# Eight one-group loads of x that leave out DMA engine 4, in place of four two-group loads

## The chip, the cores and the metric

The kernel runs on one core of a Trainium2 chip. The metric is the device time of one execution in microseconds, taken as the median of several runs. The profile is of one further execution, with its own time.

## What is computed

The input `r_inputs` has 4096 rows of 32 fields with 64 numbers each, the weights `W` one 64 x 64 matrix for each of the 496 pairs of fields i < j. All is float32. Cut to what matters, the reference is:

```python
i_idx, j_idx = np.triu_indices(32, k=1)
vi = inputs[:, i_idx, :]
vj = inputs[:, j_idx, :]
vdotw = jnp.einsum('bpd,pde->bpe', vi, W)
inter = vdotw * vj
return inter.reshape(4096, -1)
```

So each pair (i, j) yields `(x_i @ W_ij) * x_j`, 64 numbers for each row, and the output, 4096 x 31744 floats or 520 MB, is far larger than the inputs.

## The kernel before

**Tiling.** The 4096 rows are cut into 8 chunks of 512 (`BANK`). The host lays x out transposed: two fields times 64 numbers make 128 partitions, and 16 such field pairs (`NPR`) of a chunk stand side by side in `xbuf`, 512 columns each. There is one `xbuf`, used again by every chunk. It is thought of as 4 groups of 4 field pairs (`GROUP`); a group takes 8,192 bytes in each partition, 1 MB in all.

**Steps.** `steps_of` lists 124 steps a chunk. The outer order is by the group of `p`, the field pair that is multiplied by weights: group 0 has 55 steps, group 1 has 39, group 2 has 23 and group 3 has 7. Within these, the field pair `q`, which is the other factor, runs over the same and the later groups. In one step, TensorE makes two PSUM banks of 128 x 512 (L218, or L208 for the pairs inside a field pair), and VectorE multiplies them by x into an output slot in SBUF (L236, or L228). Two neighbouring steps with the same `p` are made together where PSUM and the slot have room.

**Stores.** The output goes through three slots of 20, 18 and 18 banks (`SLOTS`). A full slot is stored with one DMA from ScalarE's queue (L180), 36,864 or 40,960 bytes a partition; a slot is written again only when its store has landed on all 16 DMA engines. The weights, 8.1 MB, are loaded once at the start from the same queue.

**Loads of x.** `x_loads` lists the loads: chunk 0 comes in three (groups 0; 1; 2 and 3), every later chunk in two (groups 0 and 1; 2 and 3). The load of the next chunk into a group is issued as soon as the last step with a `p` in that group is out, since no later step of the chunk reads it: for groups 0 and 1 together after 94 steps, for 2 and 3 at the chunk's end. Most loads go out from SP (L140): one DMA of 128 partitions, 8 for each of the 16 DMA engines.

**The light loads.** `is_light` picks some loads that go out from GpSimd instead and that put no data on DMA engine 4 (`LIGHT`). `load_beside` cuts such a load in two DMAs: partitions 0 to 119 as 15 lines of 8 on the 15 engines from 5 around to 3, and partitions 120 to 127 as 2 lines of 4 on the two engines from `PAIRS_FROM[lap]` on. On the host, every line is followed by 16 floats (`PAD`). [...]`from_engine` first issues a small DMA into `nudge`:

```python
k = (e - cursor) % DMA_ENGINES
if k:
    nudge = nudges[e == LIGHT + 1]
    from_pool(nudge[:k]..., x[: k * 8]...)
cursor = e
```

So one light load is four DMAs on GpSimd's queue: nudge, 2 lines, nudge, 15 lines. All four have line L99 in the profile. `keep_in_program_order` holds them in the order in which they are written. Before, the light loads are those of groups 0 and 1 of chunks 1, 3, 5 and 7.

**What sets the order.** [...] Every DMA engine carries stores, SP's loads and GpSimd's loads.

Of the kernel before, what the change touches and what calls it, by code (L numbers as in the profile page):

```python
# [18 lines left out]

DMA_ENGINES = 16  # L20
LIGHT = 4
LIGHT_CHUNKS = [1, 3, 5, 7]
PAIRS_FROM = [7, 15, 1, 7]
HEAD = P // DMA_ENGINES
REST = HEAD // 2
PAD = 16
# [27 lines left out]
def x_loads(B, NPR):  # L54

    loads = [(0, 0, 1), (0, 1, 2), (0, 2, 4)]
    for c in range(1, B // BANK):
        loads += [(c, 0, 2), (c, 2, 4)]
    return loads


def is_light(load):

    return load[1] == 0 and load[0] in LIGHT_CHUNKS


def load_size(load):

    pads = (DMA_ENGINES + 1) * PAD if is_light(load) else 0
    return P * (load[2] - load[1]) * GROUP * BANK + pads  # L70
# [3 lines left out]
def pair_bilinear_kernel(  # L74
# [22 lines left out]
    def from_pool(out, in_):  # L97

        tc.keep_in_program_order(nc.gpsimd.dma_start(out=out, in_=in_))  # L99

    def from_engine(e):

        nonlocal cursor
# [3 lines that stand above are left out]
            from_pool(  # L107
                nudge[:k].rearrange("p (h c) -> p h c", h=2)[:, :, :4],
                x[: k * 8].rearrange("(p h c) -> p h c", p=k, h=2),
            )  # L110
        cursor = e

    def load_beside(at, xt, n_row, lap):

        nonlocal cursor
        most = DMA_ENGINES - 1
        for e, k, rows, p in (
            (PAIRS_FROM[lap], 2, REST, most * HEAD),
            (LIGHT + 1, most, HEAD, 0),
        ):  # L120
            from_engine(e)
            n = rows * n_row
            lines = x[at : at + k * (n + PAD)].rearrange("(k c) -> k c", k=k)
            from_pool(xt[p : p + k * rows], lines[:, :n])
            at += k * (n + PAD)
            cursor = (e + k) % DMA_ENGINES

    xbuf = const.tile([P, NPR * BANK], F32, tag="x", name="x")
    loads = x_loads(B, NPR)

    def load_x(load):

        at = sum(load_size(before) for before in loads[: loads.index(load)])
        c, g0, g1 = load
        n = (g1 - g0) * GROUP * BANK
        xt = xbuf[:, g0 * GROUP * BANK : g0 * GROUP * BANK + n]
        if is_light(load):
            load_beside(at, xt, n, LIGHT_CHUNKS.index(c))
        else:
            nc.sync.dma_start(out=xt, in_=x[at : at + P * n].rearrange("(p c) -> p c", p=P))  # L140

    for load in loads:
        if load[0] == 0:
            load_x(load)
# [42 lines left out]
    for c in range(NC):  # L187
        todo = list(enumerate(steps))
        while todo:
# [6 lines left out]
            n = 1  # L196
# [52 lines left out]
            for load in loads:  # L249
                if last and load[0] == c + 1 and load[2] == p // GROUP + 1:  # L250
                    load_x(load)
# [58 lines left out]
```

## Time and profile before

| | |
|---|---|
| time, median of 3 runs | 1314.06 us (1312.31 to 1315.08) |
| profiled execution: its own time | 1312.53 us |
| profiled execution: span, first to last instruction | 1310.8 us |
| busy: TensorE matmuls / weight loads | 1055.3 us (81%) / 401.3 us (31%) |
| busy: VectorE | 1152.6 us (88%) |
| busy: GpSimd | 9.4 us (1%) |
| moved by DMA | 562.39 MB, mean 429 GB/s |
| read from HBM / written to HBM | 41.68 MB / 520.09 MB |
| DMAs of x from SP / from GpSimd, nudges with them | 13 / 16 |

Shares are of the span. "DMA" in the profile is the mean busy share of the 16 DMA engines, and a DMA queue's packets are what an engine moves in one piece; here, one partition's row of a transfer. In the table of waits, a line reads: engine and instruction that waited, what ended the wait, then the total in us, the number of waits, and the longest. In the list of DMA issues, a line has what is loaded or stored, the issuing queue, the number of DMAs, the size of each in KB and the median time from issue to landing in us.

### The profile page before, as it was taken

How to read it: one execution, taken by the hardware profiler on the slowest of the kernel's cores; microseconds unless marked ns; L12 is line 12 of the kernel's file. 1: busy time of each engine (PE TensorE's matmuls, PEld its weight loads, DVE VectorE, ACT ScalarE, POOL GpSimd, SP SyncE). 2: the span in 40 equal slices, each digit the busy share in tenths (PEclk: the TensorE clock that was granted, in tenths of full speed). 3: DMA queues.
4: the chain of work that ended last, by engine and by line, in shares of the span. 5: the costliest groups of instructions: out<-in, count | busy, mean ns of one | idle time of the engine just before them, and what ended most of it. 6: DMA issues, size and time to landing. Idle time of an engine off the chain costs nothing.

```text
span 1310.8 us, 9392 instructions
## 1 busy us (share of the span) xinstructions
PE 1055.3 (81%) x4096; PEld 401.3 (31%) x4096; DVE 1152.6 (88%) x725; POOL 9.4 (1%) x20
## 2 busy tenths in 40 slices
PE   6888787988778878888778887788788788878882
PEld 2333233323323323333233332333233333323330
DVE  6999799998899879998889998899889998799993
POOL 0000000000000000000000000000000000000000
PEclk9999899998999989999999999899989999999996
DMA  9999999999999999999999999999999999999998
GB/s 390 430 432 434 422 433 430 433 431 433 432 433 433 431 432 429 433 436 429 433 434 433 433 428 424 435 434 432 432 433 434 427 427 420 430 431 437 432 433 382
DMA packets 19625, 562.39 MB, mean 429 GB/s; under 512 B 2688, under 2 KB 2688, under 8 KB 2816
## 3 DMA queue, kind: packets, MB, share of 16 engines
q10 hardware_dynamic: 16560, 528.23, 93.6%
q1 hardware_dynamic: 1872, 25.17, 4.5%
q0 software_dynamic: 1152, 8.39, 1.6%
q8 instruction: 32, 0.52, 0.1%
q14 instruction: 9, 0.07, 0.0%
HBM read 41.68 MB, written 520.09 MB: 429 GB/s over the span
## 4 chain that ended last, share of the span: by engine, by line
DMA 55%; DVE 36%; PE 5%; issue 2%; DVEq 0%
DMA out_dram<-slot 54%; DVE slot L236 32%; PE pring L218 5%; DVE slot L228 3%; PE pring L208 1%; DMA w<-in_w_dram 1%; DVEq L236 0%; DVEq L298 0%; DVEq L228 0%
## 5 line engine op out<-in xcount | busy, mean ns | idle before, releaser
L236 DVE TENSOR_TENSOR slot<-pring,x 128x1024 f32<-128x1024 f32 (+1 forms) x661 | 1077.2, 1697 | 122.8 <-DMA out_dram<-slot 81.6
L218 PE MATMUL pring<-x,w 64*128 64x512 f32 x3840 | 993.2, 626 | 216.7 <-DVE slot L236 206.6
L218 PEld LDWEIGHTS pring<-x,w 64*128 64x128 f32 x3840 | 385.5, 191 | 824.6 <-DVE slot L236 508.5
L228 DVE TENSOR_TENSOR slot<-pring,x 64x1024 f32<-64x1024 f32 x64 | 77.9, 1217 | 13.2 <-PE pring L208 12.7
L208 PE MATMUL pring<-x,w 64*64 64x512 f32 x256 | 65.4, 631 | 14.0 <-DMA w<-in_w_dram 7.4
L208 PEld LDWEIGHTS pring<-x,w 64*64 64x64 f32 x256 | 15.7, 137 | 59.4 <-DVE slot L236 26.6
L99 POOL DMA_DIRECT2D x<-in_x_dram x8 | 4.7, 586 | 1078.3 <-DVE slot L236 1078.3
L99 POOL DMA_DIRECT2D nudge<-in_x_dram x8 | 4.6, 569 | 0.9 <-POOLq L294 0.9
L294 POOL MEMSET const-bfloat16-1.0<- 128x1 bf16 x1 | 0.1, 101 | 0.0
L294 POOL MEMSET const-float32-0.0<- 128x1 f32 x1 | 0.1, 98 | 0.2 <-issue 0.2
L294 POOL MEMSET const-float32-1.0<- 128x1 f32 x1 | 0.1, 98 | 0.0
L294 POOL MEMSET const-uint8-127<- 128x1 uint8 x1 | 0.1, 98 | 0.0
## 6 DMA issues: line engine op xcount, KB each, us to landing
out_dram<-slot ACTq DMA_DIRECT2D x68, 4608.0 KB, 23.6
out_dram<-slot ACTq DMA_DIRECT2D x35, 5120.0 KB, 22.6
x<-in_x_dram SPq DMA_DIRECT2D x11, 2048.0 KB, 20.7
out_dram<-slot ACTq DMA_DIRECT2D x4, 2560.0 KB, 21.5
x<-in_x_dram POOLq DMA_DIRECT2D x4, 1920.0 KB, 31.8
out_dram<-slot ACTq DMA_DIRECT2D x2, 2048.0 KB, 22.5
w<-in_w_dram ACTq DMA_DIRECT2D x1, 2816.0 KB, 29.8
x<-in_x_dram SPq DMA_DIRECT2D x2, 1024.0 KB, 8.6
```

Of the source, the lines that this page charges most:

```text
L99: tc.keep_in_program_order(nc.gpsimd.dma_start(out=out, in_=in_))
L208: nc.tensor.matmul(pm[o * D : (o + 1) * D, ts(k, BANK)], w_sb[m * D : (m + 1) * D, s * P + k * D : s * P + (k + 1) * D], x_of(pair, m), st ...
L218: nc.tensor.matmul(pm[:, ts(2 * i + k, BANK)], w_sb[m * D : (m + 1) * D, ts(s + i, P)], x_of(p, m), start=True, stop=True,)
L228: nc.vector.tensor_tensor(strided(osb[rows, a : a + BANK], [BANK, 2]), strided(pm[rows, :BANK], [BANK, 2]), strided(x_of(p + 1 - h, h), [2 ...
L236: nc.vector.tensor_tensor(strided(osb[:, a : a + BANK], *blocks_of), strided(pm[:, :BANK], *blocks_of), strided(x_of(q), [BANK, n], [0, 2] ...
L294: nc = bacc.Bacc("TRN2", target_bir_lowering=False, num_devices=1)
```

## The change

The light loads are of one group each, and there are eight: group 0 of chunks 1 to 7, and group 1 of chunk 4. For this, groups 0 and 1 of every later chunk come in two loads. Group 0 is loaded after the 55 steps of its own group of `p`, group 1 after 94 steps as before; except for chunk 4's, group 1 is loaded from SP. The pairs of engines that take the last 8 partitions are now named for eight laps. The host's packing of x uses the same functions and follows.

```diff
 LIGHT = 4
-LIGHT_CHUNKS = [1, 3, 5, 7]
-PAIRS_FROM = [7, 15, 1, 7]
+LIGHT_LOADS = [(1, 0), (2, 0), (3, 0), (4, 0), (4, 1), (5, 0), (6, 0), (7, 0)]
+PAIRS_FROM = [7, 15, 1, 7, 15, 1, 7, 15]
...
     for c in range(1, B // BANK):
-        loads += [(c, 0, 2), (c, 2, 4)]
+        loads += [(c, 0, 1), (c, 1, 2), (c, 2, 4)]
...
 def is_light(load):
 
-    return load[1] == 0 and load[0] in LIGHT_CHUNKS
+    return load[:2] in LIGHT_LOADS
...
         if is_light(load):
-            load_beside(at, xt, n, LIGHT_CHUNKS.index(c))
+            load_beside(at, xt, n, LIGHT_LOADS.index((c, g0)))
```

On the queues: GpSimd issues 32 DMAs of x and nudges instead of 16, SP 16 loads of x instead of 13. TensorE, VectorE and ScalarE's queue keep their instructions and their order.

## Prediction

> **What bounds the kernel now.** I read the DMA rows of the page first, then its queues, its chain and its DMA issues.
>
> ```profile
> DMA  9999999999999999999999999999999999999998
> DMA packets 19625, 562.39 MB, mean 429 GB/s; under 512 B 2688, under 2 KB 2688, under 8 KB 2816
> q10 hardware_dynamic: 16560, 528.23, 93.6%
> q1 hardware_dynamic: 1872, 25.17, 4.5%
> q0 software_dynamic: 1152, 8.39, 1.6%
> DMA 55%; DVE 36%; PE 5%; issue 2%; DVEq 0%
> x<-in_x_dram SPq DMA_DIRECT2D x11, 2048.0 KB, 20.7
> x<-in_x_dram POOLq DMA_DIRECT2D x4, 1920.0 KB, 31.8
> ```
>
> The 16 DMA engines are over 90% busy in every slice but the last. Queue 10 is the stores (and w), queue 1 the x loads of SP, queue 0 those of GpSimd: 8.39 of 562.39 MB. Next the longest waits:
>
> ```profile
> POOL x L99 <- DVE slot L236: 1078.3, 4, 320.5
> DVE slot L236 <- DMA out_dram<-slot: 81.6, 48, 7.2
> ```
>
> VectorE waits for stores to free a slot; no line has an engine waiting for x. The table by stretches says how tight the DMA is. Columns: stretch, length, busy time of PE, PEld, DVE and POOL with counts, clock, DMA share, GB/s.
>
> ```profile
> 30.00:170.00 140.00, 114.76 (x449) 44.46 (x448) 124.98 (x79) 2.24 (x4) 0.94 1.00 428
> 170.00:330.00 160.00, 136.44 (x522) 52.08 (x520) 145.73 (x95) 0.00 (x0) 0.96 1.00 432
> 330.00:490.00 160.00, 130.13 (x499) 48.02 (x496) 140.90 (x89) 2.30 (x4) 0.97 1.00 432
> 490.00:650.00 160.00, 133.19 (x524) 51.10 (x524) 146.21 (x92) 0.00 (x0) 0.98 1.00 432
> 650.00:810.00 160.00, 130.80 (x514) 48.72 (x512) 144.02 (x91) 2.26 (x4) 0.98 1.00 430
> 810.00:970.00 160.00, 129.30 (x506) 50.23 (x504) 142.00 (x91) 0.00 (x0) 0.96 1.00 433
> 970.00:1130.00 160.00, 131.09 (x507) 50.24 (x507) 143.68 (x90) 1.71 (x3) 0.98 1.00 428
> 1130.00:1290.00 160.00, 129.97 (x520) 48.83 (x517) 147.28 (x93) 0.00 (x0) 0.99 1.00 433
> 1306.00:1308.00 2.00, 0.00 (x0) 0.00 (x0) 0.00 (x0) 0.00 (x0) 0.50 0.73 307
> 1308.00:1310.00 2.00, 0.00 (x0) 0.00 (x0) 0.00 (x0) 0.00 (x0) 0.50 0.13 53
> ```
>
> The share is 1.00 from 30 us on, and VectorE's last product starts at 1287.4 us (L236): the last 21 us only drain queues. So the end is set by the engine with most to move, and only three things can shift it: packet time added, packets stretched, and how evenly the engines end. Stretches with a GpSimd load (POOL count above 0) ran at 428, 432, 430 and 428 GB/s, the others at 432 to 433: those loads cost a little rate.
>
> The trace's packets give the prices. Median packet: 8,192 B 309 ns, 16,384 B 611 ns, 36,864 B 1364 ns; a completion packet 9 ns. Packets carry no engine number, but their chains (one starts 4 ns before the last ends) show all 16 engines without a pause from about 3 us, finishing between 1304.0 and 1309.5 us of the span, mean 1307.7.
>
> [...]
>
> **The change part by part.**
>
> *Relief of engine 4: nothing.* Before, each light load spares it 8 rows of 16,384 B: 4 x 8 x 0.611 = 19.6 us. After, 8 x 8 x 0.309 = 19.8 us. The need is real: in quiet 20 us stretches 10 to 16 packets exceed their median, about what one engine handles (14), by some 0.4 us together, 2% of that engine's time or about 25 us over the run. Its gap to the others would swing half as far, but all engines have one or two stores queued (a store lands after 23.6 us), so no swing of 5 us leaves any idle.
>
> *The pairs.* The last 8 rows go to two engines, 4 rows each. Before, engines 7 and 8 take two laps of 4 x 0.611 = 4.9 us in all; 15, 0, 1 and 2 take one, 2.4 us. After, at 4 x 0.309 = 1.24 us a lap: 7, 8, 15 and 0 three laps, 3.7 us; 1 and 2 two, 2.5 us. If 7 and 8 end last, the end moves by at most -0.7 us, since the third-latest chain ends 0.7 us before the last; if 15 or 0 ends last, +1.2 us. Taken: +0.2.
>
> *Smaller packets.* Seven chunks' first loads split: 7 x 128 = 896 more packets, each pair costing 2 x 309 - 611 = 7 ns more: 6.3 us over 16 engines, +0.4 us.
>
> *More transfers.* GpSimd issues 32 DMAs, not 16 (8 more nudges with 60 more engine shares, 8 more x transfers); SP 16 loads, not 13. The 16 GpSimd DMAs left 512 completion packets and 128 of 8 and 32 B; doubled, some 630 more at 9 ns, with SP's 48: 6.1 us over 16 engines, +0.4 us. Issue costs GpSimd 16 x 0.58 = 9.3 us, hidden under its 1078.3 us of waiting (uncovered, it would put a load back by 2.3 us, inside the margins below). Upper end with gaps for both items together: +1.2; lower: +0.5.
>
> *Stretched packets.* Time above the median of their kind, load and store packets together, in the four GpSimd windows: 14.8, 2.5, 8.9 and 20.1 us, 46.3 us over 16 engines = 2.9 us; SP's ten later loads average 1.0 us. For eight loads of half size no row exists. By bytes: no change. [...] By number of loads: +2.9 us. If it vanishes: -2.9. Taken: [...]-0.6.
>
> *Moved loads.* Group 0 of the next chunk is free after 55 of 124 steps, no longer 94; group 1 still after 94, groups 2 and 3 at the end. Releases come in that order, so on SP nothing stands behind a later release; on GpSimd the wait for (4,1) holds back only later nudges and loads. The tightest is (4,1): issued 30 steps before the chunk ends, first read 7 steps into the next, 37/124 x 160 = 48 us against 31.8 us to landing for twice the size. Loads of 1 MB hold up stores less at a time, so VectorE's 81.6 us may fall; worth nothing, its slack ends in the same full queues. PE, VectorE and the store order stay.
>
> Sum: 0.2 + 0.4 + 0.4 - 0.6 = **+0.4 us**. The profiled execution took 1312.53 us (span 1310.8, 1.7 around it), so 1312.9; the median is 1.5 us higher, **1314.5 us**.
>
> **The rivals.**
>
> 1. *Stretching goes by loads (slower).* Each GpSimd load upsets the engines[...], whatever its size: +2.9 + 0.8 + 0.2 = +3.9, 1318.0 us. For: the stretching comes in bursts, often at a load's start or end. Against: one load had only 2.5 us of it, so it isn't a fixed price. It decides from +1.6 us on an engine, about 9 us a load where 11.6 is today's mean.
> 2. *Stretching vanishes (faster).* -2.9 + 0.8 - 0.7 = -2.8, 1311.3 us. For: [...]the second load shows it can nearly vanish. Against: three of four did not.
> 3. *The lines miss engine 4.* If the cursor slips, engine 4 keeps up to 19.6 us. It now ends some 3 us before the last, so +17, 1331 us. Against: the same bookkeeping serves the loads now, and the cursor is counted for every transfer.
> 4. *A late load.* (4,1) on GpSimd landing after 48 us would stop PE and VectorE; with one or two stores queued, a few microseconds cost nothing.
>
> **How the numbers follow.** About 0.2% (2.6 us) is what a measurement of this kernel can tell from no change. Forecast 0.66; rival 1 0.20; rival 2 0.12; rivals 3 and 4 together 0.02. The forecast's own range is 1312.3 to 1316.6 us. The range to hold 8 in 10 takes in rival 1 and most of the way to rival 2: 1311.5 to 1318.4. Faster 0.12, same 0.66, slower 0.22.
>
> **What would show it.** After: DMA share 1.00 throughout; queue 0 still 8.39 MB; queue 1 at 25.17 MB; some 1,570 more packets; no engine waiting for x; GpSimd loads landing in under 31.8 us. Rate near 430 to 432 in every stretch says stretching by bytes or less; 428 to 429 in every one says rival 1; 433 says rival 2. Engine ends as wide as 5.5 us or narrower says the pairs behave. A wait for x, a DMA share below 1.00, or a time off by over 4 us proves the account wrong.

## The result, and the profile after

| | before | after |
|---|---|---|
| median (runs) | 1313.28 us (21) | 1315.15 us (21) |
| lowest to highest | 1311.34 to 1315.65 | 1313.61 to 1318.68 |
| profiled execution: time / span | 1312.53 / 1310.8 us | 1316.03 / 1314.2 us |

The ratio is 1.0015, interval 1.0008 to 1.0021: +1.9 us, within the 0.2% that the prediction calls no change, but on the slow side of 1 in the whole interval. The two profiled executions differ by 3.5 us, 1.6 us more than the medians do, so what is read from one execution below overstates some terms.

The first view is the page of after: its packets, queues, chain and DMA issues.

```profile
DMA  9999999999999999999999999999999999999998
DMA packets 21209, 562.39 MB, mean 428 GB/s; under 512 B 3376, under 2 KB 3376, under 8 KB 3504
q10 hardware_dynamic: 16560, 528.23, 93.5%
q1 hardware_dynamic: 2304, 25.17, 4.5%
q0 software_dynamic: 2304, 8.40, 1.6%
q8 instruction: 32, 0.52, 0.1%
DMA 52%; DVE 38%; PE 7%; issue 2%; DVEq 0%
x<-in_x_dram SPq DMA_DIRECT2D x8, 2048.0 KB, 21.6
x<-in_x_dram SPq DMA_DIRECT2D x8, 1024.0 KB, 17.9
x<-in_x_dram POOLq DMA_DIRECT2D x8, 960.0 KB, 27.5
```

Read it from the DMA row down. The engines are as full as before, queue 0 carries the same bytes, and there are 21209 - 19625 = 1,584 more packets. The light loads, half as large, land in 27.5 us where 31.8 us was shown before. The longest waits of after:

```profile
POOL x L99 <- PE pring L218: 1026.8, 8, 161.7
DVE slot L236 <- DMA out_dram<-slot: 69.7, 50, 4.2
```

VectorE waits 69.7 us for stores where it waited 81.6 us, and nothing waits for x. A reader who stopped here would expect a gain. The stretches (columns as before) say why there is none: the rate is level at 430 to 431 GB/s, no longer 428 in some and 433 in others, and the mean of the eight rows goes from 431.0 to 430.6 GB/s. That is 0.1%, or some 1.2 us over 1,260 us: as much as is in question here, and less than rounded figures can settle.

```profile
30.00:170.00 140.00, 115.88 (x458) 43.63 (x460) 127.42 (x82) 2.23 (x4) 0.98 1.00 431
170.00:330.00 160.00, 133.74 (x522) 52.22 (x518) 145.82 (x94) 2.29 (x4) 0.97 1.00 431
330.00:490.00 160.00, 130.88 (x496) 49.34 (x498) 140.63 (x88) 2.27 (x4) 0.96 1.00 430
490.00:650.00 160.00, 130.68 (x518) 51.50 (x516) 144.36 (x91) 4.54 (x8) 0.98 1.01 431
650.00:810.00 160.00, 129.29 (x508) 48.88 (x505) 142.24 (x90) 2.26 (x4) 0.98 1.00 430
810.00:970.00 160.00, 131.78 (x506) 50.90 (x503) 141.94 (x91) 2.24 (x4) 0.95 1.00 431
970.00:1130.00 160.00, 133.13 (x512) 51.09 (x510) 143.59 (x90) 1.75 (x3) 0.97 1.00 430
1130.00:1290.00 160.00, 135.24 (x526) 51.76 (x524) 148.15 (x94) 0.00 (x0) 0.97 1.00 431
```

More of the time went in the tail, where only stores drain. In steps of 2 us, the last two columns being DMA share and GB/s, after ends so:

```profile
1306.00:1308.00 2.00, 0.00 (x0) 0.00 (x0) 0.00 (x0) 0.00 (x0) 0.50 0.80 340
1308.00:1310.00 2.00, 0.00 (x0) 0.00 (x0) 0.00 (x0) 0.00 (x0) 0.50 0.31 131
1310.00:1312.00 2.00, 0.00 (x0) 0.00 (x0) 0.00 (x0) 0.00 (x0) 0.50 0.24 102
1312.00:1314.00 2.00, 0.00 (x0) 0.00 (x0) 0.00 (x0) 0.00 (x0) 0.50 0.03 12
```

One engine is a share of 0.06. The 0.24 to 0.31 between 1308 and 1312 us are four or five engines still at work while the rest are done; before had 0.13 from 1308 us and then nothing. The chains of packets (one packet starts 4 ns before the last of its engine ends) give each engine's end: in after four engines end between 1311.7 and 1312.7 us, the other twelve by 1310.0. Which packets belong to which engine follows from the chains and from the number of rows that each transfer gives an engine. Where two chains meet they can be exchanged, so a single engine's sums are good to some tenths of a us; the ends don't depend on it.

From the chains I made one sum for every kernel: the mean of the 16 ends, how far the last end lies above it ("lead"), and the time that packets took above the median of their size after 30 us ("stretch"). It is divided by where it falls: in GpSimd's own x packets, and around SP's loads of x (SP's own packets, and the stores in the same windows, from a load's first row to its last with a margin of about 1.5 us).

| profiled execution | mean end | lead of the last | stretch per engine | in GpSimd's x packets, sum | around SP's loads, sum |
|---|---|---|---|---|---|
| before | 1307.7 us | 1.8 us | 6.5 us | 22.1 us | 10.6 us |
| after | 1309.1 us | 3.6 us | 7.2 us | 0.1 us | 52.3 us |

So the last end, 3.2 us later, is 1.4 us of mean and 1.8 us of lead. At median packet times alone an engine is busy 0.8 us longer, and the stretch adds 0.7 us. The stretch has moved: GpSimd's 8,192 B packets have none of what its 16,384 B packets had, but around SP's loads there is five times as much. With the stores beside them, GpSimd's loads had 46 us before and 17 us after. So stretch went from one kind of load to the other, 29 us less and 42 us more. It sits in few packets: after has 50 stores lengthened by over 300 ns in the windows of 13 SP loads, before 7 in 10; one took 2,881 ns for 40,960 B, where 1,514 ns is the median.

It is also spread unevenly, and an engine that is never idle (the DMA share is 1.00 or 1.01 in the eight rows above) ends later by all the stretch that it meets. One engine stands apart, the one that takes no light rows: 25.7 us of stretch before and 25.9 after, some 20 us above the mean of the others, which is what the relief takes off it. Of the other fifteen, each had 1.8 to 6.7 us before and has 3.0 to 9.8 after. The four that end last in after are the four with most, 8.8 to 9.8 us. Three of them have no extra rows, the very last among them. The fourth has extra rows in three laps (a lap is one light load's turn of the pairs); its partner in the same pair ends at 1307.2 us, with 3.0 us of stretch.

### The profile page after: what moved, and what is told of

Read it like the earlier page. It is cut to its first block, busy times and chain, and to the rows that moved or that the text cites. A ratio compares the mean times of both kernels' runs of the same rounds, so it can differ in the third digit from the quotient of the medians.

```text
span 1314.2 us, 9431 instructions
## 1 busy us (share of the span) xinstructions
PE 1060.5 (81%) x4096; PEld 406.7 (31%) x4096; DVE 1153.9 (88%) x725; POOL 18.5 (1%) x36
## 2 busy tenths in 40 slices
DMA packets 21209, 562.39 MB, mean 428 GB/s; under 512 B 3376, under 2 KB 3376, under 8 KB 3504
## 4 chain that ended last, share of the span: by engine, by line
DMA 52%; DVE 38%; PE 7%; issue 2%; DVEq 0%
DMA out_dram<-slot 51%; DVE slot L236 34%; PE pring L218 6%; DVE slot L228 3%; PE pring L208 1%; DMA w<-in_w_dram 1%; DVEq L236 0%; DVEq L298 0%; DVEq L228 0%
## 5 line engine op out<-in xcount | busy, mean ns | idle before, releaser
L236 DVE TENSOR_TENSOR slot<-pring,x 128x1024 f32<-128x1024 f32 (+1 forms) x661 | 1078.5, 1699 | 125.5 <-DMA out_dram<-slot 69.7
L218 PEld LDWEIGHTS pring<-x,w 64*128 64x128 f32 x3840 | 390.9, 193 | 823.0 <-DVE slot L236 500.7
L99 POOL DMA_DIRECT2D x<-in_x_dram x16 | 9.4, 587 | 1026.8 <-PE pring L218 1026.8
L99 POOL DMA_DIRECT2D nudge<-in_x_dram x16 | 9.0, 564 | 0.9 <-POOLq L294 0.9
## 6 DMA issues: line engine op xcount, KB each, us to landing
out_dram<-slot ACTq DMA_DIRECT2D x35, 5120.0 KB, 23.7
x<-in_x_dram POOLq DMA_DIRECT2D x8, 960.0 KB, 27.5
```

The costliest lines, as they stand in the source:

```text
L218: nc.tensor.matmul(pm[:, ts(2 * i + k, BANK)], w_sb[m * D : (m + 1) * D, ts(s + i, P)], x_of(p, m), start=True, stop=True,)
L236: nc.vector.tensor_tensor(strided(osb[:, a : a + BANK], *blocks_of), strided(pm[:, :BANK], *blocks_of), strided(x_of(q), [BANK, n], [0, 2] ...
```

## The experiments

Two things could have made the time beyond the added packets: uneven rows, that is, which engines get the extra rows of the light loads; or the stretch around the loads, and then the size of a light load, its start after 55 steps, the split of SP's loads, or where lines lie in memory. Each measured ratio is to the kernel before, with its interval. The last two columns are sums over all engines, with the stores in the same windows.

| kernel | ratio | light loads | lead | stretch per engine | around GpSimd's loads | around SP's loads |
|---|---|---|---|---|---|---|
| after | 1.0015 (1.0008 to 1.0021) | one group | 3.6 us | 7.2 us | 17 us | 52.3 us |
| e1_pairs_spread | 1.0028 (1.0017 to 1.0039) | one group | 4.0 us | 6.9 us | 15 us | 48.1 us |
| e2_pairs_one | 1.0064 (1.0050 to 1.0079) | one group | 5.4 us | 9.5 us | 25 us | 81.3 us |
| g1_pairs_elsewhere | 1.0036 (1.0023 to 1.0048) | one group | 5.1 us | 7.3 us | 25 us | 48.3 us |
| e4_same_bytes | 1.0031 (1.0020 to 1.0042) | one group | 5.5 us | 6.4 us | 21 us | 37.8 us |
| k1_group_1 | 1.0019 (1.0013 to 1.0026) | one group | 2.5 us | 6.5 us | 13 us | 48.8 us |
| f1_pad_4096 | 1.0023 (1.0013 to 1.0034) | one group | 5.4 us | 6.9 us | 16 us | 49.3 us |
| e3_before_spread | 1.0009 (1.0001 to 1.0017) | two groups | 4.5 us | 7.6 us | 51 us | 20.7 us |
| k2_before_one_pair | 1.0028 (1.0019 to 1.0038) | two groups | 5.1 us | 6.0 us | 27 us | 23.7 us |
| f3_split_alone | 1.0009 (1.0001 to 1.0017) | two groups | 3.0 us | 6.1 us | 42 us | 10.1 us |
| f4_before_pad | 1.0001 (0.9992 to 1.0010) | two groups | 2.6 us | 6.2 us | 34 us | 17.2 us |
| f2_no_relief | 1.0092 (1.0075 to 1.0110) | none | 7.3 us | 9.4 us | none | 101.6 us |

Leads and sums are of one execution each; only their large differences are read. The seven kernels with one-group light loads lie at 37.8 us and more around SP's loads, the five with two-group loads (the kernel before is the fifth) at 23.7 us and less. Around GpSimd's loads it is the other way round: 25 us and less against 27 us and more. The whole stretch doesn't follow the time: e4 and k1 have no more of it than the kernel before, 6.5 us, and are slower. So the move by itself doesn't make the time; the lead has to be read beside it.

**Uneven rows.** `e1_pairs_spread` is after with its extra rows given to different engines.

```diff
-PAIRS_FROM = [7, 15, 1, 7, 15, 1, 7, 15]
+PAIRS_FROM = [7, 9, 11, 13, 15, 1, 5, 2]
```

> The changed kernel, with the eight 2-line transfers on eight different pairs of engines (7, 9, 11, 13, 15, 1, 5, 2): no engine but engine 2 takes more than one lap of 4 x 0.309 = 1.24 us, where 7, 8, 15 and 0 took three (3.7 us). Evenness theory (the four engines with three laps end last): the four latest ends come down 2.5 us, others rise by up to 1.2, so the end falls by 1.5 to 2 us against the changed kernel, to about 1313.3 us, ratio to the kernel before 0.999 to 1.001; the engines end closer together than 6.0 us. Stretching theory (each GpSimd load or its place in time costs rate): no change, ratio 1.0015, 1315.2 us.

It was 1316.51 us, no faster than after. Spreading the extra rows gained nothing. `e2_pairs_one` gives all of them to engines 7 and 8.

```diff
-PAIRS_FROM = [7, 15, 1, 7, 15, 1, 7, 15]
+PAIRS_FROM = [7, 7, 7, 7, 7, 7, 7, 7]
```

> The changed kernel, with all eight 2-line transfers on engines 7 and 8: 8 x 1.24 = 9.9 us there in place of 3.7. Evenness theory: the end rises by up to 6.2 us against the changed kernel, to about 1321 us, ratio 1.005 to 1.0065, and two engines end some 6 us or more after the rest. Stretching theory: 1315.2 us, ratio 1.0015.

It was 1321.76 us, 6.6 us over after, where five more laps ask for 6.2 us on these two engines. Its tail, in steps of 4 us:

```profile
1312.00:1316.00 4.00, 0.00 (x0) 0.00 (x0) 0.00 (x0) 0.00 (x0) 0.50 0.33 139
1316.00:1320.00 4.00, 0.00 (x0) 0.00 (x0) 0.00 (x0) 0.00 (x0) 0.50 0.07 31
```

A share of 0.07 over 4 us is two engines at work for about half of it. The chains show which: the two that took 12 rows in every lap end at 1318.3 and 1319.3 us, the others by 1315.4. So extra rows are priced rightly, and `from_engine` does steer them: its `cursor` is the kernel's own count of the engine on which GpSimd's next transfer starts, and by it the lines of 4 rows of all eight laps fell on the same two engines, which end 2.9 us and more after the others.

`e3_before_spread` did to the kernel before what e1 did to after, and `k2_before_one_pair` what e2 did:

```diff
-PAIRS_FROM = [7, 15, 1, 7]
+PAIRS_FROM = [7, 15, 1, 9]
```

> The kernel before with its fourth lap on engines 9 and 10, not again on 7 and 8: the most that an engine takes falls from 4.9 to 2.4 us. Evenness theory: 0.5 to 2 us faster than before, ratio 0.9985 to 0.9996; in the records of before no two engines stand out at the end, so the small end is likelier. Stretching theory: ratio 1.0000.

1314.39 us, slower by 0.0001 to 0.0017, where a gain was expected.

```diff
-PAIRS_FROM = [7, 15, 1, 7]
+PAIRS_FROM = [7, 7, 7, 7]
```

> The kernel before with all four 2-line transfers on engines 7 and 8: 9.8 us of extra rows there in place of 4.9, all else as before, two-group loads. Evenness: those two end last, up to 4.9 us later, ratio 1.002 to 1.004. Stagger theory (engines out of step lengthen packets around x loads): stores and x rows in SP's windows lengthened by 25 us or more in sum, where before had 11; if they stay near 11, it is one-group light loads that lengthen them and not lag as such.

1317.26 us: two engines end 3.7 and 5.1 us above the mean, which is what two more laps of 4 x 0.611 = 4.9 us for 7 and 8 ask for. The second question, whether engines that lag make packets longer around SP's loads, was answered only in part: 23.7 us, above the 10.6 of before, below the 25 asked for and less than half of after. Last of this kind, `g1_pairs_elsewhere` takes the extra rows off engines 7, 8, 15 and 0, in case these are slower by themselves.

```diff
-PAIRS_FROM = [7, 15, 1, 7, 15, 1, 7, 15]
+PAIRS_FROM = [9, 11, 13, 1, 5, 9, 11, 13]
```

> The changed kernel with the pairs on engines 9, 11, 13, 1, 5, 9, 11, 13 and the one after each: 7, 8, 15 and 0 take no extra rows, 9 to 14 two laps (2.5 us). In the records of the changed kernel and of the two pairs runs the latest engines were ones with laps on 7 or 8 and with 7 to 9 us of stretching where others had 3 to 6. Theory of slow engines (7 and 8 lose more time whatever their share, so extra rows belong elsewhere): the last end comes down 2 us or more, ratio 0.9995 to 1.0005. Evenness by rows alone: 1.2 us less than the changed kernel, ratio 1.0005. Neither: 1.0015 to 1.003.

1317.89 us: that idea falls; in k2, too, engines 7 and 8 have 1.6 and 3.3 us of stretch, under its mean of 6.0.

But e1, e3 and g1 are no clean tests of evenness, since engines carry more than rows of x and stores. The 32 instruction fetches (queue 8 of the profile), with a median of 0.93 us in after, lie on eight engines, four on each: 3.7 us, and some 1.6 us of stretch on the packets beside them. In the chains of after and k2 no fetch lies on the engine without light rows or on one with extra rows. Engines 7, 8, 15, 0, 1 and 2, which take the extra rows of before and after, are all without fetches. In e1 the six engines of the laps from 9, 11 and 13 on have four fetches each. So these three runs moved rows onto the fuller engines. In e3 the last two ends, 1312.0 and 1313.2 us, are the engines of its fourth lap, 9 and 10. In g1 eight engines end between 1309.9 and 1314.4 us and the other eight by 1308.4; the last two laps, from 11 and from 13, are on engines of the late half. An uneven share cost what its rows cost (6.6 us for 6.2 in e2); whether an even share of all packets would bring even ends was not run.

**Size, start and split.** `e4_same_bytes` is after with the bytes of before: both groups of chunks 1, 3, 5 and 7 light, each engine with as many bytes of light rows as in before.

```diff
-LIGHT_LOADS = [(1, 0), (2, 0), (3, 0), (4, 0), (4, 1), (5, 0), (6, 0), (7, 0)]
-PAIRS_FROM = [7, 15, 1, 7, 15, 1, 7, 15]
+LIGHT_LOADS = [(1, 0), (1, 1), (3, 0), (3, 1), (5, 0), (5, 1), (7, 0), (7, 1)]
+PAIRS_FROM = [7, 7, 15, 15, 1, 1, 7, 7]
```

> Eight one-group light loads, but in the chunks and groups of before (0 and 1 of chunks 1, 3, 5 and 7), with pairs 7, 7, 15, 15, 1, 1, 7, 7, so that every engine moves the same bytes as before: 4.9 us for 7 and 8. What differs from before is packet size, number of transfers and that group 0 comes earlier. Evenness theory: against before only the added 0.8 us, ratio 1.0006 (1314.1 us); against the changed kernel 7 and 8 have 1.2 us more, so up to 1316.4 us. Stretching theory: as the changed kernel, ratio 1.0015, since the number of GpSimd loads is the same.

1317.34 us. `f3_split_alone` makes the same split of SP's loads, in chunks 2, 4 and 6, and leaves the light loads of the kernel before as they are.

```diff
-        loads += [(c, 0, 2), (c, 2, 4)]
+        loads += [(c, 0, 2), (c, 2, 4)] if c in LIGHT_CHUNKS else [(c, 0, 1), (c, 1, 2), (c, 2, 4)]
```

> The kernel before, but in chunks 2, 4 and 6 groups 0 and 1 come in two loads from SP. The four two-group light loads stay as they were. By the sum of the prediction: 384 packets and 3 transfers more, 0.2 us, ratio 1.0002. If splitting in itself (earlier, smaller loads) lengthens stores, the ratio is 1.001 or more.

1313.87 us: +1.2 us by the ratio (interval from 0.1 us; 0.9 us in the medians), where 0.2 was expected, with the stretch of before: 8 lengthened stores around 13 SP loads. Its time does not separate it from after; its stretch does. Against e4 it separates both: these two differ only in the light loads, eight of one group (group 0's issued after 55 steps) against four of two, with the same bytes for every engine, and their intervals do not meet. So one-group light loads cost some 0.0022 or 2.9 us there. By counts and medians 0.6 us of it are added packets. In the profiled pair the stretch per engine is 0.3 us more and the lead 2.5 us more: most of it is uneven ends, on the same bytes.

`k1_group_1` then asks whether it is the size of a light load or its early start. Its light loads have the size of after's, but nearly all are of group 1 and start where before's did, after 94 steps; group 0 comes from SP.

```diff
-LIGHT_LOADS = [(1, 0), (2, 0), (3, 0), (4, 0), (4, 1), (5, 0), (6, 0), (7, 0)]
+LIGHT_LOADS = [(1, 1), (2, 1), (3, 1), (4, 0), (4, 1), (5, 1), (6, 1), (7, 1)]
```

> The changed kernel with group 1 light instead of group 0 in chunks 1, 2, 3, 5, 6 and 7: the same sizes, numbers, pairs and bytes of every engine, but GpSimd's loads start after 94 steps, as those of before did, and SP's one-group loads after 55. Time theory (GpSimd's early start costs): ratio 1.0006. Size theory (one-group light loads cost whenever they run): 1.0015 to 1.003, stores in SP's windows lengthened by 25 us or more in sum, the last engine 3.5 us or more above the mean.

1315.81 us, with an interval above the 1.0006 that an early start would have left, and 48.8 us around SP's loads: the small light loads cost this, not their early start. Whether it is their size or that there are eight of them isn't separated, since the bytes are the same. The lead, 2.5 us, stayed under the 3.5 expected. `h1_held`, e4 with group 0's load held back to 94 steps and put behind group 1's, was meant to ask the same.

```diff
-            for load in loads:
-                if last and load[0] == c + 1 and load[2] == p // GROUP + 1:
+            for load in reversed(loads):
+                if last and load[0] == c + 1 and max(load[2], 2) == p // GROUP + 1:
```

> As e4_same_bytes (eight one-group light loads in chunks 1, 3, 5 and 7, bytes of each engine as before), but group 1's load stands ahead of group 0's on both queues, so both start after 94 steps as the two-group load of before did. What is left of the change is packet size and the number of transfers alone. Time theory (the earlier start of group 0 costs): ratio 1.0006, the 0.8 us of added packets. Size theory (one-group GpSimd loads cost, whenever they run): as e4_same_bytes, ratio 1.002 to 1.004, stores in SP's windows lengthened by 25 us or more in sum where before had 7, the last engine 3.5 us or more above the mean.

1344.12 us, ratio 1.0237 (1.0218 to 1.0256): it became another experiment. In its table of waits TensorE waits for x, as in no other kernel:

```profile
POOL nudge L99 <- DMA nudge<-in_x_dram: 94.7, 7, 16.7
DVE slot L228 <- PE pring L208: 89.1, 7, 20.4
PE pring L208 <- DMA x<-in_x_dram: 71.3, 4, 19.3
```

Two light loads stand back to back on GpSimd. The nudge tile of the second is in use until the first's nudge has landed, so GpSimd waits up to 16.7 us (e1 and g1, with their other pairs, have one such wait of 13 us, hidden). Group 0's x is then late, TensorE stands, and VectorE behind it. This is the late load of the prediction's fourth rival, seen at work: about 31 us. On size and start it says nothing.

**Where lines lie in memory.** `f1_pad_4096` and `f4_before_pad` set the lines of a light load in HBM 4,096 B apart instead of 64, in after and in before.

```diff
-PAD = 16
+PAD = 1024
```

> The changed kernel with PAD = 1024 floats, so that every line and every load of x starts at a multiple of 4,096 bytes in HBM; before, each light load moves the later ones on by 1,088 bytes, and the changed kernel has eight such shifts where before had four. Alignment theory (SP's 2 MB loads lengthen the stores because x lies askew: 1 to 3 us a load before, 1.5 to 13 us after, growing with the chunk): stretching in SP's windows falls back to 1 us a load, mean -2 us, ratio 1.000. Stagger theory (engines out of step meet more often, wherever x lies): no change, ratio 1.0015 to 1.003.

> The kernel before with PAD = 1024 floats. Alignment theory: the stretching in its windows falls, 1 to 2 us faster, ratio 0.9985 to 0.999. Stagger theory: 1.000.

1316.69 and 1313.02 us: no gain in either, and 49.3 us around SP's loads in f1. Alignment falls. f4 is the fastest variant that was run and is not distinct from the kernel before; none beats it.

**No relief.** `f2_no_relief` is after with every load from SP.

```diff
-LIGHT_LOADS = [(1, 0), (2, 0), (3, 0), (4, 0), (4, 1), (5, 0), (6, 0), (7, 0)]
-PAIRS_FROM = [7, 15, 1, 7, 15, 1, 7, 15]
+LIGHT_LOADS = []
+PAIRS_FROM = []
```

> The changed kernel without light loads: all x comes from SP, no load leaves out engine 4, no GpSimd transfer runs. Rival 3's price: engine 4 has 19.8 us more, and the others 1.3 us less, so it ends last, 14 to 20 us later than the changed kernel: 1329 to 1335 us, ratio 1.012 to 1.017. Stagger theory: with engine 4 far behind, stores in SP's windows are lengthened by 25 us or more in sum; if they are near the 7 us of before, it takes one-group GpSimd loads to lengthen them.

1325.81 us, 10.7 us over after, where 14 to 20 were expected, and 11.8 us over the kernel before. Its tail:

```profile
1312.00:1316.00 4.00, 0.00 (x0) 0.00 (x0) 0.00 (x0) 0.00 (x0) 0.50 0.65 277
1316.00:1320.00 4.00, 0.00 (x0) 0.00 (x0) 0.00 (x0) 0.00 (x0) 0.50 0.05 23
1320.00:1324.00 4.00, 0.00 (x0) 0.00 (x0) 0.00 (x0) 0.00 (x0) 0.50 0.03 14
```

A single engine, a share of 0.05, is at work to 1322.4 us, 7.7 us after all others. So the relief is worth about 11 us in the form of after and 12 us in that of before. There is no transfer from GpSimd here, and still the most stretch around SP's loads, 101.6 us in 21 windows (4.8 a window; after 4.0, before 1.1). So it needs no light load. That it needs engines out of step fits this run, but isn't shown.

## Why the prediction was right, and where it was off

The time fell in the forecast's range, but the sum was less good than the number. It asked for +0.4 us and +1.9 us were measured, about midway between the forecast and rival 1. The forecast of 1314.5 us came closer, to 0.7 us, because it stood on a first median of before that lay 0.8 us above the later one: that part is luck.

**The bound and the cover: right.** DMA is full in every slice but the last, no engine waits for x, queue 0 carries the same bytes, and there are 1,584 more packets against some 1,570. VectorE's wait for stores fell by 11.9 us and moved nothing, as said.

**Smaller packets and more transfers: right.** +0.4 and +0.4 us predicted; by the counts and medians of after's packets, +0.8 us an engine.

**Stretched packets: mis-sized, with the sign wrong.** Taken at -0.6 us, the author's estimate; measured at +0.7 in the profiled pair. In the GpSimd windows, which the step counted, stretch fell by 1.8 us an engine, from 46 us in sum to 17: three times the estimate, less than in rival 2, which was right for GpSimd's own packets (22.1 us went to 0.1). But the step took the stores around SP's loads as fixed at 1.0 us a load. There it came back: 10.6 us to 52.3, 2.6 us an engine. The test by rate, 430 to 432 in every stretch for "by bytes or less", came out as written, and was blind to this: it sums over both places. Rival 1, a price for each GpSimd load, has the sign of the result but not the place. What stretches a packet was not shown: the runs here tell how much and beside which loads, not by what.

**The ends: mis-sized, and the step that was off most.** The prediction said that how evenly the engines end can shift the time, but gave this term to the rows of the pairs alone, +0.2 us, and divided the stretch evenly over 16 engines. The lead of the last engine rose by 1.8 us in the profiled pair, and the ends of after lie 6.0 us apart, over the 5.5 that was to show that the pairs behave. The extra rows were counted rightly, as e2 and k2 show by 6.6 and 4.0 us, and 15 and 0, which were feared, end at 1307.4 and 1308.1 us. What set the last end was the stretch of single engines: 9.8 us on the last, without extra rows, where no engine but the relieved one had over 6.7 us before. The 3.7 us of fetches on eight engines, which even out against the extra rows of the pairs, were not in the working either.

**Relief at nothing: right on average.** Engine 4 shows in the chains, since some 90% of its stores are about 28 ns longer than the median; in after it takes no row of GpSimd's loads, so rival 3 is out, and it ends 0.9 us after the median engine, not last.

Open is why one-group light loads move the stretch to the stores around SP's loads, and why it falls on few engines. Shown is that it goes with loads of one group (k1, and e4 against f3), and that a run with one lagging engine and no light load has twice as much of it (f2); e2 has it too, and k2, with two lagging engines, has less than half. Whether the first works through the second, and on which side of the engines, was not settled. Of the +1.9 us, 0.8 is counted work. The other 1.1 is stretch and lead together, and their shares differ from execution to execution: with the extra rows on the engines without fetches, the three profiles with two-group loads (before, f3, f4) have 6.1 to 6.5 us of stretch and leads of 1.8 to 3.0 us, the four with one-group loads (after, e4, k1, f1) 6.4 to 7.2 and 2.5 to 5.5.

## What to carry to other kernels

Where the DMA engines are full to the end, split the time in three before costing an edit: packets at their median, packets above it, and the lead of the last engine, each from the chains of single engines. Count everything that an engine carries before calling a share even, instruction fetches too (3.7 us on each of eight engines here). A change that leaves the bytes and the mean rate alone (431.0 to 430.6 GB/s) can still move the third (1.8 to 3.6 us), and equal bytes are no promise of equal ends (e4: a lead of 5.5 us). Small helper transfers have buffers too: two loads back to back can wait for the landing of one (h1: up to 16.7 us).

## What was not expected of the hardware

- One engine of 16 was slower on nearly every store, about 28 ns of 1,364, or 25 us over the run; without relief this cost only 11.8 us over the kernel before.
- In GpSimd's loads, packets of 16,384 B were stretched by up to 610 ns (before), those of 8,192 B by at most 24 (after), beside the same stores; in e1 one of these took 523 ns more, in e2 they add up to 7.1 us, in g1 to 4.0.
- The 32 instruction fetches of 16,384 B took 0.93 to 0.97 us each on average, where a row of x of that size takes 0.611, and lay on the same eight engines, four on each.
